# Layer 0 of a graph-attention stack: list and own row of groups 1 to 3 are put in rank order by one indirect transfer out of SBUF

## The chip, the cores and the metric

The kernel runs on one core of a Trainium2 chip. The metric is the device time of one execution in microseconds. Engines are called as in the profile: PE (TensorE), DVE (VectorE), ACT (ScalarE), POOL (GpSimd) and SP (SyncE, which here only issues transfers).

## The reference, cut to what matters

There are 3327 nodes with 256 features and a sparse adjacency matrix, 3327 x 3327 int32, with about 1% of ones and a full diagonal. Four attention layers follow each other, each as `x = layernorm(x + gnn(x, adj))`. Only layer 0 matters here; its scores are not a sum of a row term and a column term, so each pair of neighbours is scored on its own:

```
g_src = x @ W_src.T + b_src                        # one row per node
g_tgt = x @ W_tgt.T + b_tgt
score[i, j] = sum_c a[c] * leaky_relu(g_src[i, c] + g_tgt[j, c])
weights = softmax over j of score, where adj[i, j] != 0
x = layernorm(x + weights @ g_tgt)
```

## The kernel before

**Sparse layer 0.** The function `sparse0` scores a node only against its neighbours. For each node it makes a list of the neighbours' indices (at most 56, `KMAX`), and it then fetches the neighbours' `g_tgt` rows from a table in DRAM, `table_d` (260 numbers a row, 130 KB for 128 nodes), with an indirect transfer on POOL: one instruction fetches one neighbour for each of 128 nodes. This is `gather`, L721, 945 instructions.

**Groups and ranks.** The 26 tiles of 128 nodes are divided into four groups of 4, 7, 9 and 6 tiles (`SETS`). Inside a group the nodes are sorted by their number of neighbours, so that the first tile of a group needs 56 gathers and the last ones fewer than 30 (`LEVELS`). The generator `neighbours(s)` makes the lists of a group: SP loads pieces of the adjacency (`adj_i`, 512 KB, three buffers), ACT converts them (`adj_b`, L484), PE turns them into codes (`v`), DVE takes the largest codes (`cand`, `found`, L514 to L524), and `note` writes a payload of 58 numbers per node: the list, the node's own index in the group, and its diagonal entry. A count of larger keys gives each node's rank, `ranks_i`. It also calls `sources`, which writes the negative `g_src` row of each node.

**Own rows.** Next to the list, each node has an own row of 773 numbers (`OWN`) in `own_d`, in the order of the nodes: the negative `g_src` row, x, and `g_tgt`. Three places write it: `targets`, `sources` and a copy of x.

**Into rank order.** For group 0, `permute` sorts the lists with matmuls. For groups 1 to 3, POOL writes each tile's payload to its ranks in `lists_d` with an indirect transfer (`write_list`, L665), and loads all lists of the group back (`read_lists`, L673). Own rows stay where they are: for each tile in rank order `gather_own` (L709, POOL, 26 instructions) fetches the 128 own rows by the index in the list.

**What is done with them.** `lay_out` copies the own `g_src` row to PSUM (`minus_ps`, ACT). `score` (DVE, L741 and L747) scores up to four neighbours at once. `weights` makes the softmax weights. `combine` scales the gathered rows (ACT, L794) and adds them up on PE (L797), which frees the gather's buffer. `add_input` adds x. `put_back` (POOL, L834) writes the sum to the node's place in `sums_d`, and `take` loads it.

**Order.** Gathers are cut into parts of up to 4; there are 245 parts. The program goes through the parts in steps, one for each part q. POOL's gathers of part q + 8 (`LEAD`) are written beside the scores of part q, and there are 22 buffers of four rows (`TURNS`). `at_step(q, f)` puts f at step q. `once_placed(q, f)` puts f where the gathers of part q are written. `owed` spreads the making of the next group's lists over the steps before. Group 1 starts at part 41, group 2 at part 106 and group 3 at part 188. Work in the list `between` (the list writes and the sums) is taken one piece after every second gather. The order on PE, DVE, ACT and POOL is the order of the program. The order on SP is chosen when the kernel is built. Each engine issues in its own order, and an instruction whose wait isn't over holds what is behind it.

## Time and profile before

| | |
|---|---|
| median of 3 runs | 3092.57 us (3083.05 to 3094.05) |
| the profiled execution, its own time | 3086.17 us |
| its span, first to last instruction | 3084.3 us |
| busy time of PE, DVE, ACT, POOL | 2371.3, 2131.5, 872.9, 1017.5 us |
| layer 0: first and last gather of POOL | 145.8 and 1440.0 us |
| POOL's instructions there: gathers, own gathers, list writes, list loads, sums | 945, 26, 22, 3, 26 |

The profile shows one execution. A line of a group names the source line, the engine, the operation, output<-input, how often, then busy time and mean ns of one, then the idle time of the engine just before these instructions and what ended it. A transfer's instruction ends when it is issued; its landing is told apart, as the time from issue to landing. "issue" means that the engine waited for nothing that the profile shows.

### The profile page before, as it was taken

What the parts mean: (1) busy time and instruction counts of PE and PEld (TensorE: products, weight loads), DVE (VectorE), ACT (ScalarE), POOL (GpSimd) and SP (SyncE); (2) the same over time, 40 slices, a digit from 0 to 9 for tenths busy, and PEclk for the clock granted to TensorE, in tenths of its full rate; (3) what the DMA queues carried; (4) which work ended last, traced back from release to release, by engine and by line L of the source; (5) the groups of instructions that cost most, each with busy time, mean ns of one, the idle gap of its engine ahead of it and who ended that gap; (6) DMA issues with size and microseconds to landing.
All of it is one profiled execution on the core that took longest, in us unless ns stands there. A gap on an engine that the chain in (4) does not pass through costs nothing.

```text
span 3084.3 us, 45518 instructions
## 1 busy us (share of the span) xinstructions
PE 2371.3 (77%) x16077; PEld 1302.9 (42%) x16098; DVE 2131.5 (69%) x5525; ACT 872.9 (28%) x2426; POOL 1017.5 (33%) x1073
## 2 busy tenths in 40 slices
PE   5747657544456432646799999989999999999996
PEld 2313223222222111313688888874434545434332
DVE  3499997776778536654355531129888889899997
ACT  2226545433344322535234421110110110120110
POOL 0077777777777777775000000000000000000000
PEclk8657868776777666868999999999999999999998
DMA  6676675455644435543776643331212212212211
GB/s 181 178 186 189 190 177 171 128 139 147 151 127 116 114 105 118 138 109 95 231 247 204 198 122 92 106 124 46 70 43 72 70 45 71 67 46 61 57 47 45
DMA packets 193029, 372.04 MB, mean 121 GB/s; under 512 B 38992, under 2 KB 135201, under 8 KB 191770
## 3 DMA queue, kind: packets, MB, share of 16 engines
q1 hardware_dynamic: 107648, 176.03, 20.1%
q0 software_dynamic: 51520, 156.84, 19.8%
q10 hardware_dynamic: 33626, 36.18, 3.4%
q8 instruction: 130, 2.13, 0.3%
q14 instruction: 105, 0.86, 0.1%
HBM read 326.21 MB, written 46.12 MB: 121 GB/s over the span
## 4 chain that ended last, share of the span: by engine, by line
PE 46%; DVE 4%; DMA 2%; issue 0%; ACT 0%; SPq 0%; POOL 0%; DVEq 0%; POOLq 0%; ACTq 0%
PE acc L1493 18%; PE acc L1446 16%; PE acc L1501 9%; PE misc L1292 3%; DVE e L1362 2%; DMA at<-at_d 1%; DMA at_i<-in_adj_t_dram 0%; PE misc L1389 0%; PE misc L1575 0%; PE misc L1536 0%; DMA dst<-in_l_a_dram 0%; DVE stats L1653 0%; DVE h L1651 0%; DVE both L1648 0%; DVE h L248 0%
## 5 line engine op out<-in xcount | busy, mean ns | idle before, releaser
L721 POOL DMA_INDIRECT g<-table_d,lst x945 | 900.4, 953 | 306.8 <-issue 255.5
L1362 DVE SCALAR_TENSOR_TENSOR e<-rate,feat,at 128x896 f32<-128x896 f32 (+4 forms) x832 | 843.9, 1079 | 80.9 <-PE acc L1501 70.0
L797 PE MATMUL acc<-g,ident 128*128 128x512 f32 x958 | 524.7, 694 | 341.8 <-ACT g L794 299.5
L1493 PE MATMUL acc<-e,feat 128*32 128x384 f32 (+2 forms) x6656 | 690.2, 516 | 7.3 <-DVE h L1466 4.5
L797 PEld LDWEIGHTS acc<-g,ident 128*128 128x128 f32 x958 | 205.1, 224 | 577.9 <-ACT g L794 442.9
L741 DVE TENSOR_TENSOR y<-g,minus_ps 128x1028 f32<-128x1028 f32 (+2 forms) x245 | 288.9, 1179 | 220.0 <-DMA g<-table_d,lst 203.2
L1493 PEld LDWEIGHTS acc<-e,feat 128*32 128x32 f32 x6656 | 258.4, 110 | 347.6 <-issue 235.8
L794 ACT ACTIVATE g<-g,w 128x256 f32<-128x256 f32 x945 | 389.1, 495 | 16.0 <-issue 8.6
L1501 PE MATMUL acc<-e,feat 128*32 128x384 f32 (+3 forms) x3328 | 376.0, 512 | 0.0
L747 DVE SCALAR_TENSOR_TENSOR y<-y,a_ps 128x257 f32<-128x257 f32 x945 | 342.7, 418 | 7.5
L1446 PE MATMUL acc<-feat,e 128*128 128x257 f32 (+2 forms) x1352 | 304.1, 382 | 15.5 <-DMA at_i<-in_adj_t_dram 13.2
L1446 PEld LDWEIGHTS acc<-feat,e 128*128 128x128 f32 (+2 forms) x1352 | 255.4, 191 | 53.3 <-issue 14.2
L242 POOL TENSOR_TENSOR rstds<-rstds,minus_half 128x7 f32<-128x7 f32 (+1 forms) x12 | 19.7, 1645 | 775.9 <-DVE rstds L241 775.9
L494 PE MATMUL v<-code,leads 65*128 65x512 bf16 (+1 forms) x182 | 84.2, 464 | 221.0 <-DVE cand L514 178.4
L1446 PE MATMUL acc<-feat,at 128*128 128x257 bf16 (+2 forms) x2028 | 237.8, 274 | 4.2 <-DMA at<-at_d 4.0
L1446 PEld LDWEIGHTS <-at 128*128 128x128 bf16 (+2 forms) x2028 | 198.8, 99 | 37.9 <-DMA at<-at_d 4.5
L1501 PEld LDWEIGHTS acc<-e,feat 128*32 128x32 f32 (+1 forms) x3328 | 139.0, 110 | 154.8 <-issue 131.2
L514 DVE MAX8 cand<-v 128x8 f32<-128x104 f32 (+2 forms) x858 | 159.1, 259 | 53.5 <-PE v L497 41.4
L1362 DVE SCALAR_TENSOR_TENSOR e<-rate,feat,at_i 128x896 f32<-128x896 f32 (+2 forms) x104 | 111.6, 1080 | 73.3 <-DMA at_i<-in_adj_t_dram 51.9
L1342 POOL DMA_DIRECT2D rate3b_d<-rate_rows x4 | 2.1, 526 | 468.9 <-ACT rate_rows L1341 468.9
L494 PEld LDWEIGHTS <-leads 65*128 65x128 bf16 x182 | 19.8, 109 | 287.2 <-DVE cand L514 232.4
L1379 ACT CAST at<-at_i 128x896 bf16<-128x896 int32 (+2 forms) x104 | 92.0, 885 | 107.8 <-DMA at_i<-in_adj_t_dram 90.0
(201 smaller groups left out, 1788.3 us busy)
## 6 DMA issues: line engine op xcount, KB each, us to landing
adj_i<-in_adj_dram SPq DMA_DIRECT2D x75, 512.0 KB, 4.4
at<-at_d SPq DMA_DIRECT2D x150, 224.0 KB, 2.5
at_i<-in_adj_t_dram SPq DMA_DIRECT2D x50, 448.0 KB, 4.5
g<-table_d,lst POOLq DMA_INDIRECT x945, 2.8
at<-at_d SPq DMA_DIRECT2D x75, 192.0 KB, 2.3
at<-at_d SPq DMA_DIRECT2D x75, 191.8 KB, 2.3
at_d<-at ACTq DMA_DIRECT2D x50, 224.0 KB, 4.2
at_i<-in_adj_t_dram SPq DMA_DIRECT2D x25, 384.0 KB, 3.3
```

Of the source, the lines that this page charges most:

```text
L494: nc.tensor.matmul(v[:, :w], leads[:, b, :], code[:, :w], start=True, stop=False)
L514: nc.vector.max(spread[:, c0 + c, :], view(v[:, :w]))
L721: nc.gpsimd.indirect_dma_start(out=g[:, k - k0, :], out_offset=None, in_=table_d[:, :], in_offset=bass.IndirectOffsetOnAxis(ap=entry["lst" ...
L741: nc.vector.tensor_tensor(y, rows, minus_src[:, None, :].to_broadcast([P, m, dim + 1]), op=ALU.max)
L747: nc.vector.scalar_tensor_tensor(y, y, 1.0, a_ps[:, : dim + 1], op0=ALU.mult, op1=ALU.mult, accum_out=sc)
L794: nc.scalar.activation(rows, rows, AF.Copy, scale=w[:, k : k + 1])
L797: nc.tensor.matmul(dst, ident, rows, start=start, stop=stop)
L1292: nc.tensor.matmul(pacc[:pn, : dim + self.extra], ht[:, k, :pn], self.weight[:, k, :], start=(k == 0), stop=(k == kc - 1),)
L1362: nc.vector.scalar_tensor_tensor(e[:pn, : c1 - c0], self.rate[b][:pn, h_of, : c1 - c0], q, at[:pn, : c1 - c0], op0=ALU.max, op1=ALU.mult,)
L1446: nc.tensor.matmul(accs[s][:pn, : dim + 1], a[:pj, s * P : s * P + pn], f[:pj, : dim + 1], start=(j == 0 and part == 0), stop=(j == nt - 1 ...
L1493: nc.tensor.matmul(accs[x][p][q : q + 32, : hi - lo], f[:pj, at0 : at0 + 32], es[at0 // hd][:pj, lo:hi], start=(j == 0), stop=(j == nt - 1),)
L1501: nc.tensor.matmul(accs[x][pairs][h_of * 32 : (h_of + 1) * 32, : hi - lo], f[:pj, dim + h_of : dim + h_of + 1].to_broadcast([pj, 32]), es[ ...
```

## The change

The payload of groups 1 to 3 no longer goes to its rank by itself. `note` writes it (from ACT) behind the node's own row in `own_d`, whose rows grow from 773 to 831 numbers. `write_list` becomes two halves: SP loads a whole tile of 128 rows of 831 numbers into a tile `stage` in SBUF (two buffers), and POOL writes this tile to its ranks in `lists_d` with one indirect transfer; the load of tile t is written one piece of `between` ahead of the write of tile t. `read_lists` is issued by SP and loads the lists as floats into a buffer of the same two (`read`), and a new `keep_lists` on ACT converts them. `gather_own` becomes a plain load of 128 consecutive rows by SP for groups 1 to 3; group 0 keeps its four indirect gathers. The payload has 3 buffers instead of one per tile, and `own` has 3 instead of 4. The list writes start two steps earlier than before, and the load of the lists one step.

The diff:

```diff
@@ -44,6 +44,7 @@
 AT_X = 257
 AT_TGT = 513
 OWN = 773
+AT_LIST = OWN
 
 
 @with_exitstack
@@ -366,7 +367,7 @@
             own_d = []
             for s, size in enumerate(SETS):
                 lo, hi = starts[s] * P, min(n, (starts[s] + size) * P)
-                own_d.append(dram.tile([size * P, OWN], F32, name=f"own{s}_d"))
+                own_d.append(dram.tile([size * P, OWN if s == 0 else AT_LIST + KMAX + 2], F32, name=f"own{s}_d"))
                 if s == 0:
                     copy_rows(nc.gpsimd, own_d[s][: hi - lo, AT_X : AT_X + dim], x[lo:hi, :])
 
@@ -403,7 +404,7 @@
                 yield
                 nc.scalar.copy(row[:pn], pt[:pn, :ROW])
                 nc.scalar.dma_start(table_d[1 + it * P : 1 + it * P + pn, :], row[:pn])
-                nc.scalar.dma_start(own_rows(it)[:, AT_TGT:], row)
+                nc.scalar.dma_start(own_rows(it)[:, AT_TGT:OWN], row)
                 yield
 
             def sources(it):
@@ -422,7 +423,7 @@
                 yield
 
             lists_d = [
-                dram.tile([size * P, KMAX + 2], U32, name=f"lists{s}_d")
+                dram.tile([size * P, AT_LIST + KMAX + 2], F32, name=f"lists{s}_d")
                 for s, size in enumerate(SETS)
             ]
             sums_d = [
@@ -529,7 +530,7 @@
                 def note(t):
                     it, found = starts[s] + t, founds.pop(t)
                     payload = io0.tile(
-                        [P, KMAX + 2], U32 if s else F32, tag=f"pay{t}", name="payload", bufs=1
+                        [P, KMAX + 2], F32, tag=f"pay{t}" if s == 0 else "pay", name="payload", bufs=1 if s == 0 else 3
                     )
                     nc.vector.tensor_scalar(
                         payload[:, :KMAX], found, 1.0 - BASE, 0.0, op0=ALU.add, op1=ALU.max
@@ -542,6 +543,8 @@
                         junk, found, BASE - 0.5, 0.0, op0=ALU.is_lt, op1=ALU.add,
                         accum_out=missing,
                     )
+                    if s:
+                        nc.scalar.dma_start(own_d[s][t * P : (t + 1) * P, AT_LIST:], payload)
 
                 def key(t):
                     it = starts[s] + t
@@ -660,20 +663,35 @@
                 )
                 listed[0] = lst
 
+            staged = {}
+
             def write_list(s, t):
-                ranks_i, payloads = placed[s]
-                nc.gpsimd.indirect_dma_start(
-                    out=lists_d[s][:, :],
-                    out_offset=bass.IndirectOffsetOnAxis(ap=ranks_i[:, t : t + 1], axis=0),
-                    in_=payloads[t][:, :], in_offset=None,
-                )
+                if t < SETS[s]:
+                    stage = staged[s, t] = io0.tile([P, AT_LIST + KMAX + 2], F32, tag="stage", name="stage")
+                    nc.sync.dma_start(stage, own_d[s][t * P : (t + 1) * P, :])
+                if t:
+                    ranks_i, _ = placed[s]
+                    nc.gpsimd.indirect_dma_start(
+                        out=lists_d[s][:, :],
+                        out_offset=bass.IndirectOffsetOnAxis(ap=ranks_i[:, t - 1 : t], axis=0),
+                        in_=staged.pop((s, t - 1))[:, :], in_offset=None,
+                    )
 
             def read_lists(s):
+                while between:
+                    between.pop(0)()
+                read = io0.tile([P, AT_LIST + KMAX + 2], F32, tag="stage", name="read")
+                read = read[:, : max(SETS) * (KMAX + 2)].rearrange("p (t k) -> p t k", k=KMAX + 2)
+                nc.sync.dma_start(
+                    read[:, : SETS[s], :],
+                    lists_d[s].rearrange("(t p) k -> p t k", p=P)[:, :, AT_LIST:],
+                )
                 lst = io0.tile([P, max(SETS), KMAX + 2], U32, tag="lst", name="lst")
-                nc.gpsimd.dma_start(
-                    lst[:, : SETS[s], :], lists_d[s].rearrange("(t p) k -> p t k", p=P)
-                )
                 listed[s] = lst
+                return read
+
+            def keep_lists(s, read):
+                nc.scalar.copy(listed[s][:, : SETS[s], :], read[:, : SETS[s], :])
 
 
             pens = {}
@@ -705,7 +723,10 @@
 
                 entry = held[s, t] = {"g": {}}
                 lst = entry["lst"] = listed[s][:, t, :]
-                own = entry["own"] = io0.tile([P, OWN], F32, tag="own", name="own_of", bufs=4)
+                own = entry["own"] = io0.tile([P, OWN], F32, tag="own", name="own_of", bufs=3)
+                if s:
+                    nc.sync.dma_start(own, lists_d[s][t * P : (t + 1) * P, :OWN])
+                    return
                 nc.gpsimd.indirect_dma_start(
                     out=own[:, :], out_offset=None, in_=own_d[s][:, :],
                     in_offset=bass.IndirectOffsetOnAxis(ap=lst[:, KMAX : KMAX + 1], axis=0),
@@ -979,9 +1000,11 @@
                 if k0 == 0:
                     if key[1] == 0:
                         at_step(q, judge, key[0])
-                        at_step(q, lay_out, *key)
+                        if key[0]:
+                            once_placed(q - 2, gather_own, *key)
+                        at_step(q - 2 if key[0] else q, lay_out, *key)
                     else:
-                        once_placed(q - 3, gather_own, *key)
+                        once_placed(q - 2, gather_own, *key)
                         at_step(q - 2, lay_out, *key)
             for q, key in ends.items():
                 count = len(cuts_of(places[key]))
@@ -1013,9 +1036,12 @@
             ahead, owed, steps = [], {}, 0
             for s in range(1, len(SETS)):
                 at = begins[s] - LEAD - 2
-                at_step(at, read_lists, s)
+                reads = {}
+                at_step(at - 1, lambda s, reads: reads.update({s: read_lists(s)}), s, reads)
+                at_step(at, lambda s, reads: keep_lists(s, reads[s]), s, reads)
+                at -= 2
                 at -= SETS[s] // 2 + 1
-                for it in range(SETS[s]):
+                for it in range(SETS[s] + 1):
                     at_step(at, between.append, lambda s=s, it=it: write_list(s, it))
                 ahead.append(neighbours(s))
                 steps += steps_of(s)
```

More of the change, by code (lines that the diff above doesn't have):

```diff
@@ L661, in permute, with read_lists @@
                 listed[0] = lst
+            staged = {}
             def write_list(s, t):
-                ranks_i, payloads = placed[s]
-                nc.gpsimd.indirect_dma_start(
-                    out=lists_d[s][:, :],
-                    out_offset=bass.IndirectOffsetOnAxis(ap=ranks_i[:, t : t + 1], axis=0),
-                    in_=payloads[t][:, :], in_offset=None,
+                if t < SETS[s]:
[8 more added lines that the diff above has]
+                    )
+            def read_lists(s):
+                while between:
[5 more added lines that the diff above has]
+                    lists_d[s].rearrange("(t p) k -> p t k", p=P)[:, :, AT_LIST:],
                 )
-            def read_lists(s):
                 lst = io0.tile([P, max(SETS), KMAX + 2], U32, tag="lst", name="lst")
-                nc.gpsimd.dma_start(
-                    lst[:, : SETS[s], :], lists_d[s].rearrange("(t p) k -> p t k", p=P)
-                )
                 listed[s] = lst
+                return read
+            def keep_lists(s, read):
+                nc.scalar.copy(listed[s][:, : SETS[s], :], read[:, : SETS[s], :])
             pens = {}
```

## The prediction

> **What bounds the kernel now.** I read the slices first, then the costly groups, then GpSimd's own groups, and last the timeline around one step that the change touches.
>
> ```profile
> PE   5747657544456432646799999989999999999996
> POOL 0077777777777777775000000000000000000000
> DMA  6676675455644435543776643331212212212211
> ```
>
> A slice is 77 us. POOL shows a flat 7 from slice 2 to slice 17, and that plateau is layer 0. The later layers belong to PE and the change does not touch them.
>
> ```profile
> L721 POOL DMA_INDIRECT g<-table_d,lst x945 | 900.4, 953 | 306.8 <-issue 255.5
> L741 DVE TENSOR_TENSOR y<-g,minus_ps 128x1028 f32<-128x1028 f32 (+2 forms) x245 | 288.9, 1179 | 220.0 <-DMA g<-table_d,lst 203.2
> ```
>
> 945 gathers of 953 ns stand 0.30 us apart, and that gap is called "issue": POOL waits for nothing. VectorE waits for the gathers, not they for it. From 145.8 to 1441 us the end of layer 0 is therefore a count of POOL's instructions, 1.26 us each. The groups of POOL say what the others cost:
>
> ```profile
> L834 POOL DMA_INDIRECT sums_d<-hs,lst x26 | 26.2, 1009 | 30.1 <-DVE lost L1048 12.9 <-DVE inv L821 9.9 <-issue 4.3
> L709 POOL DMA_INDIRECT own_of<-own_d,lst x26 | 25.0, 961 | 134.4 <-DVE lst L658 126.9 <-issue 7.2 <-DVE y L741 0.3
> L665 POOL DMA_INDIRECT lists_d<-payload,ranks_i x22 | 22.2, 1007 | 10.4 <-DMA lists_d<-payload,ranks_i 5.2 <-issue 5.2
> L673 POOL DMA_DIRECT2D lst<-lists_d x3 | 3.1, 1030 | 0.0
> ```
>
> An own row is three times as long as a gathered row, yet costs POOL the same. In the third line, 5.2 us of waits for an earlier list write already stand. The timeline of POOL at the end of group 1's writes shows one, and the list's load:
>
> ```profile
> 344.76 0.99 POOL L665 DMA_INDIRECT lists_d<-payload,ranks_i  x1 [0.30 <-issue]
> 346.06 0.97 POOL L721 DMA_INDIRECT g<-table_d,lst  x1 [0.30 <-issue]
> 347.34 0.96 POOL L721 DMA_INDIRECT g<-table_d,lst  x1 [0.31 <-issue]
> 349.19 0.99 POOL L665 DMA_INDIRECT lists_d<-payload,ranks_i  x1 [0.89 <-DMA lists_d<-payload,ranks_i]
> 350.49 0.97 POOL L721 DMA_INDIRECT g<-table_d,lst  x1 [0.30 <-issue]
> 351.77 0.96 POOL L721 DMA_INDIRECT g<-table_d,lst  x1 [0.31 <-issue]
> 352.73 1.08 POOL L673 DMA_DIRECT2D lst<-lists_d  x1
> ```
>
> Unhindered, write follows write after 3.83 us (1.01 + 0.30 and two gathers); here it took 4.43, because the write before had not landed. Landing times, of the own rows, the list writes and the sums in turn, are in the answers by tile:
>
> ```profile
> DMA to landing us min/median/max: 3.7/4.0/6.3
> DMA to landing us min/median/max: 2.2/2.3/5.4
> DMA to landing us min/median/max: 2.4/2.5/9.3
> ```
>
> And two waits, SP's for ScalarE's conversion of the adjacency and VectorE's for gathers, inside the stretch from 130 to 1420 us:
>
> ```profile
> SPq L126 <- ACT adj_b L484: 481.4, 64, 45.4
> DVE y L741 <- DMA g<-table_d,lst: 189.6, 85, 9.5
> ```
>
> **What the Trainium skill says.** "Perfetto Trace Analysis", section "DMA Instruction — SWDGE (GPSIMD)": the profile ends such an instruction when the descriptors are made, not when data has landed. The trace agrees: 961 ns for own rows (386 KB), 953 for gathers (130 KB). So I price the larger list write at 1.01 us of POOL too. "DMA: Bandwidth & Descriptors", section "Anatomy of one DMA — SWDGE (gpsimd) path": 2.0 us plus bytes/436e3 per transfer. For the list write (29 KB) and the sums (128 KB) the fit gives 2.1 and 2.3 us against 2.3 and 2.5 measured; for an own row it gives 2.9 against 4.0, so for large rows I use the trace. Its section "Rules for kernel authors" says that a DMA reading what another wrote must wait for that one's completion, and that spreading transfers over issuing engines adds no bandwidth. The first is L665's wait above; the second no run here shows alone.
>
> **The change part by part.** The sum is made against the profiled execution: 3086.17 us with a span of 3084.3. The median of the runs is 3092.57, 6.4 higher, so I carry a difference over.
>
> Removed from POOL. The built order has 22 own gathers fewer (group 0 keeps its four): 22 x 1.26 = 27.7 us. Three list loads leave: from 351.77 the next gather would have come at 353.03 and came at 354.11, 1.08 each, 3.2 us. The waits of L665 beyond plain issue are 5.2 - 5 x 0.30 = 3.7 us; I take them out to count all waits anew. Gross: 34.6 us, all on the path.
>
> Added on POOL. The 22 list writes stay, two gathers apart, but each now moves 128 x 831 x 4 bytes = 416 KB instead of 29. Each waits for the write before it to land and for its stage, which SP loads. There are two stage buffers, so SP's load for write k+2 waits for write k to land. In the built order the first two stages of each group are loaded far ahead; the third needs the first write. So a loop of write, landing, load, landing spans two writes. Write landing: extrapolating list to sums (0.2 us for 99 KB) gives 3.1, the own gather with 30 KB more gives 4.1; I take 4.1, since rows of this length landed so. Load: adjacency pieces land in 2.5 us at 127.5 KB and 4.4 at 512 KB, interpolated 3.9; around 300 to 360 us the large ones took 5.0, so 4.5 there. With two wake-ups of 0.25 us the loop is 8.5 to 9.1 us, 4.3 to 4.6 a write. Chance delays, such as the list writes' 5.4, are added to a wait and never subtracted: I take 4.7, so 0.9 above 3.83. The first write of each group waits for none of this: 19 x 0.9 = 17 us. Bounds: below, 3.1 + 3.7 + 0.5 = 7.3 per pair, no stall, 0 us. Above, per write two gathers, a write, a load and half an adjacency piece are 1347 KB; the stretch 146 to 1441 moved 144 GB/s at a DMA share of 0.55, so 262 GB/s when busy: 5.3 us. With queueing 5.7, a stall of 1.9, is 36 us. A gain from the larger write itself is excluded: its descriptors are as many as before.
>
> Added on SP: 22 stage loads, 22 own loads, three list loads, each an issue of about 0.4 us, of no account by itself. But SP issues in order. The third stage load of group 2 stands ahead of three adjacency pieces which before were issued at 640.1, 643.7 and 658.8; they now wait for writes that begin near 665. What is late next is scanning of group 3's adjacency, on ScalarE, PE and VectorE. POOL's cover is the gather buffers: 22, filled 8 parts ahead.
>
> Added on ScalarE: three copies of the list (under 1 us), 22 payload issues, and the wait of that copy. It stands at step 96 for group 2. ScalarE was through with that step at 660.4; the last write would be at about 702 (nine, 4.7 apart), landed at 706, loaded at 711. ScalarE stands some 50 us, and with it VectorE from about 671 to 713, because the next tile's `minus` and the conversions are queued behind the copy. VectorE had some 25 us of work there. From 720 to 800 it was busy 58.6 of 80 us, so it catches up 21; 4 remain at the end of the group's first tile. POOL's own margin: the first part of that tile was scaled at 801-802, its buffer was wanted 31 us later, at 833.6. In group 1 the hold is about 330 to 354, margin 28 us; group 3's falls on 28.6 us for which VectorE stood already (1114 to 1143). So I cost the hold at nothing, covered by those margins; if cover is gone, it costs POOL what exceeds them.
>
> POOL's first gather of a new group now waits for the copy: write, load and copy need some 10 us after the last write; 13, 11 and 16 gathers and some sums lie between (14 us at least). Own rows for later tiles come ahead on SP with 3 buffers instead of 4; the shortest tiles make that load wait for `add_input` three tiles back, at most five steps of 5 us, needed eight steps later. Nothing.
>
> Sum: -34.6 + 17 = -17.6 us, 3068.6 against 3086.17; on the median about 3076.
>
> **The rivals.** (a) No stall: landings fit under two gathers. For it, the small list writes waited only 5 times in 22; against it, 14 times the bytes. -34.6: 3058. (b) The DMA engines are the bound in the write windows: 36 us of stalls eat the gain. For it, DMA shares of 0.54 in the first window before anything is added; against it, 0.44 and 0.33 in the other two. About +1: 3094. (c) Slower: SP's queue becomes the releaser. Between the stage loads of groups 1 and 2 stand eight adjacency or x pieces, and a wait of SP for a conversion is 481.4/64 = 7.5 us on average. Each piece that holds a stage beyond the landing it overlaps (about 1.5 us spare) costs POOL 6 us: 8 x 6 = 48, so +30: 3122. It decides from about 2 us per piece for the gain to vanish, 4 us for a measurable loss. Against it: ScalarE and VectorE run ahead of POOL in the program, and SP reached those pieces before the writes. A hold of ScalarE past the margins adds to the same side. That the change does not do what it says can be left out: the built order shows the 22 gathers gone.
>
> **How the numbers follow.** A measurement of this kernel can tell about 0.5%, 15.5 us. Case (a) 0.15, faster. My case 0.45: stalls of 8 to 27 us, gain 8 to 27, two thirds of it beyond 15.5, so 0.30 faster and 0.15 same. Case (b) 0.20, same. Case (c) 0.20, slower. Together 0.45, 0.35, 0.20. The range runs from (a) with 3 us of scatter in the runs, 3055, to half of (c), 3108; my case alone is 3065 to 3085.
>
> **What would show it.** Right: POOL's groups list 4 own gathers; the list write's idle time is 10 to 30 us, released by the stage or by the earlier write; gathers keep 0.30 us; POOL's last gather comes near 1424 instead of 1440; ScalarE waits some 50 us for `read`. Wrong: list writes waiting over 2 us each, a stage load released by ScalarE rather than by a write, gathers waiting for PE (a full ring of buffers), or a first gather waiting for the list's copy.

## The result, and the profile after

The kernel after takes 3089.07 us (median of 12 executions, 3078.82 to 3105.65), the kernel before 3091.97 (12 executions): ratio 0.999, 95% interval 0.9975 to 1.0005. The forecast was 3076, a gain of 16 us; what came is 3 us between the medians, and the interval runs from a gain of 8 us to a loss of 1.5.

The first measurement and the last series of experiments found the kernel before at 3090 us, the four series between them at 3513 to 3536 us, so kernels are compared only within their series, and the two levels are kept apart by these numbers.

The profiled execution of after took 3105.65 us (span 3103.9), the longest of its 12. Its groups on GpSimd, in the form line, engine, operation, tiles, count, then busy time and mean ns of one, then idle time in front of them and what ended it:

```profile
L742 POOL DMA_INDIRECT g<-table_d,lst x945 | 897.7, 950 | 322.2 <-issue 255.7 <-DMA g<-table_d,lst 25.9 <-DMA table_d<-row 19.6
L674 POOL DMA_INDIRECT lists_d<-stage,ranks_i x22 | 21.9, 996 | 35.5 <-DMA lists_d<-stage,ranks_i 31.3 <-issue 2.7 <-DVE ranks_i L619 1.6
L730 POOL DMA_INDIRECT own_of<-own_d,lst x4 | 3.9, 976 | 143.7 <-DVE lst L661 137.1 <-DVE hs L844 6.0 <-issue 0.6
```

The work removed is gone: four own gathers are left of 26, and no list load. One list write costs GpSimd 996 ns, as before (1007), though it moves 416 KB and not 29. But the idle time in front of the 22 writes rose from 10.4 to 35.5 us, and 31.3 of it ended when an earlier list write landed. The third line holds a second new wait: 6.0 us of an own gather for `hs`. The timeline of GpSimd near the end of group 1's writes (start, duration, engine, line, idle time before) shows what the writes look like:

```profile
363.74 0.99 POOL L674 DMA_INDIRECT lists_d<-stage,ranks_i  x1 [0.62 <-DMA lists_d<-stage,ranks_i]
365.03 0.97 POOL L742 DMA_INDIRECT g<-table_d,lst  x1 [0.30 <-issue]
366.31 0.95 POOL L742 DMA_INDIRECT g<-table_d,lst  x1 [0.30 <-issue]
371.23 0.99 POOL L674 DMA_INDIRECT lists_d<-stage,ranks_i  x1 [3.97 <-DMA lists_d<-stage,ranks_i]
372.53 0.97 POOL L742 DMA_INDIRECT g<-table_d,lst  x1 [0.30 <-issue]
373.80 0.95 POOL L742 DMA_INDIRECT g<-table_d,lst  x1 [0.30 <-issue]
376.31 0.99 POOL L674 DMA_INDIRECT lists_d<-stage,ranks_i  x1 [1.56 <-DMA lists_d<-stage,ranks_i]
```

From write to write 7.49 and 5.08 us, where two gathers and a write need 3.83. Over all pairs within a group the mean distance is 5.39 us (4.04 before). The landing of these writes, in the answer by their line, was 2.2/2.3/5.2 before (the 5.4 that the prediction names is from a view that takes in the list loads too) and is now:

```profile
DMA to landing us min/median/max: 3.2/4.9/6.4
```

Three waits bear on the other steps of the prediction (waiting engine and line, what it waits for, total us, times, longest; SP's queue is SPq):

```profile
ACT lst L694 <- DMA read<-lists_d: 126.6, 3, 61.4
POOL g L742 <- PE acc L818: 9.7, 32, 0.3
SPq L671 <- DMA lists_d<-stage,ranks_i: 181.7, 16, 67.9
```

ScalarE does stand at the list's copy, up to 61.4 us. GpSimd does not feel it: its 32 waits for a gather buffer are of 0.3 us, which is plain issue. SP's stage loads stand for the landing of list writes, not for ScalarE's conversions (two more waits of theirs, 15.1 us together, are for a payload to land in `own_d`).

**The balance from first to last gather** (idle time beyond 0.30 us per instruction counted as wait) comes out of the timelines of GpSimd. The stretch ends where the last gather starts, and that gather is still counted among the instructions, so instructions and waits together exceed it by some 1.2 us. The waits include small negative terms, of instructions that follow with less than 0.30 us, so the columns to their right can exceed them. The last two rows are kernels of the experiments below. All four are at 3090 us:

| kernel | first gather at | stretch | instructions with 0.30 us each | waits | of list writes | of gathers | of own gathers |
|---|---|---|---|---|---|---|---|
| before | 145.8 | 1294.2 | 1283.6 | 11.8 | 3.8 | 9.7 | 0.0 |
| after | 161.7 | 1300.7 | 1248.7 | 53.3 | 28.9 | 19.4 | 5.7 |
| after_c (after again) | 139.9 | 1296.2 | 1248.9 | 48.6 | 28.3 | 15.1 | 5.9 |
| gross_order | 149.8 | 1264.5 | 1248.9 | 16.8 | 5.2 | 12.3 | 0.0 |

35 us of instructions left, 37 to 42 us of waits came. Some 3 of the 35 us are not instructions removed: the gathers took 950 ns each instead of 953 in the lower three kernels, which nobody had forecast and nothing here explains. In the same three kernels 1.3 us of the list writes' waits, at the first write of group 1, are for `ranks_i`; the rest is for landings. That the first gather came at 161.7 in the first profile is no part of the change: the same kernel had it at 139.9 in another execution, and the kernel before had it at 160.8 in one (before_p, below).

### The profile page after: what moved, and what is told of

It reads as the page before. It is cut to its first block, busy times and chain, and to the rows that moved or that the text cites. A ratio compares the mean times of both kernels' runs of the same rounds, so it can differ in the third digit from the quotient of the medians.

```text
span 3103.9 us, 45643 instructions
## 1 busy us (share of the span) xinstructions
PE 2369.9 (76%) x16076; PEld 1305.4 (42%) x16098; DVE 2130.2 (69%) x5525; ACT 872.3 (28%) x2429; POOL 990.0 (32%) x1048
## 4 chain that ended last, share of the span: by engine, by line
PE 46%; DVE 4%; DMA 1%; issue 1%; ACT 0%; SPq 0%; POOL 0%; DVEq 0%; POOLq 0%
PE acc L1519 18%; PE acc L1472 16%; PE acc L1527 9%; PE misc L1318 2%; DVE e L1388 2%; DMA at<-at_d 1%; PE misc L1415 0%; PE misc L1601 0%; PE misc L1562 0%; DMA dst<-in_l_a_dram 0%; DMA at_i<-in_adj_t_dram 0%; DVE stats L1679 0%; DVE h L1677 0%; DVE both L1674 0%; DVE h L249 0%
## 5 line engine op out<-in xcount | busy, mean ns | idle before, releaser
L818 PE MATMUL acc<-g,ident 128*128 128x512 f32 x958 | 508.4, 675 | 446.6 <-ACT g L815 394.9
L818 PEld LDWEIGHTS acc<-g,ident 128*128 128x128 f32 x958 | 198.8, 217 | 673.4 <-ACT g L815 545.4
L485 ACT ACTIVATE adj_b<-adj_i 128x1024 bf16<-128x1024 int32 (+1 forms) x104 | 92.3, 888 | 148.1 <-issue 55.5
```

Of the source, the lines that this page charges most:

```text
L485: nc.scalar.activation(adj_b[:pn, : hi - lo], loaded.pop((t, p))[:pn, : hi - lo], AF.Copy, accum_out=counts[:pn, it, p : p + 1],)
L818: nc.tensor.matmul(dst, ident, rows, start=start, stop=stop)
```

## The experiments

Theory: where GpSimd is the bound, the 35 us of its instructions are really saved, and come back as waits of the list writes, of one own gather and of some gathers. Rivals: GpSimd's instruction count is not what ends layer 0; ScalarE's hold costs the time; the stage loads or SP's queue, not the landing, slow the writes.

### First series (before at 3513.14 us)

**after_again** is the changed kernel unaltered.

> The changed kernel once more, unaltered, for a second profile beside the runs of this series. Theory: the 31 us of GpSimd instructions that left (22 own gathers, three list loads) are saved, and come back on GpSimd as waits: list writes waiting for the write before them or their stage about 25 to 30 us beyond plain issue (28.9 in the first profile against 3.6 before), the own gather of group 0's last tile waiting about 6 us for `hs` (3 own buffers), gathers waiting for earlier transfers 5 to 15 us. First to last gather then 1290 to 1302 us, time 3080 to 3100. The late first gather of the first profile (161.7 us against 145.8) is the granted clock of TensorE in the first 160 us, not the change: with another clock there it should come at another time, 140 to 165. Rival: the late start belongs to the change, and comes again at 160 or later whatever the clock.

3465.28 us, ratio 0.986 (0.9831 to 0.9888). First gather at 154.9. The expected times were missed by far, because layer 0 ran otherwise here. Three views tell how: the group of gathers in this kernel, a line of VectorE's timeline in the kernel before at 3090 us, and VectorE's timeline in this kernel at 247 us:

```profile
L742 POOL DMA_INDIRECT g<-table_d,lst x945 | 897.4, 950 | 523.7 <-issue 293.9 <-PE acc L818 153.6 <-remote 21.5
```

```profile
199.90 1.63 DVE L514 MAX8 cand<-v 128x8 f32<-128x104 f32 x9
```

```profile
248.65 0.28 DVE L515 MAX8 cand<-v 128x8 f32<-128x104 f32 x1 [1.11 <-issue]
250.06 0.28 DVE L515 MAX8 cand<-v 128x8 f32<-128x104 f32 x1 [1.13 <-issue]
251.45 0.28 DVE L515 MAX8 cand<-v 128x8 f32<-128x104 f32 x1 [1.11 <-issue]
252.86 0.27 DVE L515 MAX8 cand<-v 128x8 f32<-128x96 f32 x1 [1.13 <-issue]
```

Where nine such instructions took 1.63 us before, one of 0.28 us starts every 1.4 us here, without a wait that the profile shows. TensorE and ScalarE start late too, while GpSimd goes on at 1.26 us per gather until its buffers are full and it stands for TensorE (153.6 us; 9.7 in the first profile). So here the other engines set the pace of layer 0. GpSimd waits 393.4 us in the stretch, and 411.0 in the kernel before at this level (before_p, below). List writes still waited 24.8 us for landings.

**noown**, in the kernel before:

```diff
                 own = entry["own"] = io0.tile([P, OWN], F32, tag="own", ...)
+                if s:
+                    nc.sync.dma_start(own, own_d[s][t * P : (t + 1) * P, :])
+                    return
```

> The kernel before, with one edit: the own rows of groups 1 to 3 are loaded by SyncE in node order instead of gathered by GpSimd in rank order (so the own rows belong to other nodes than the lists: part of the computation is changed). List writes, list loads and all buffers are those of before. It shows what the removal of 22 own gathers is worth when nothing is added to GpSimd. Theory (the end of layer 0 is a count of GpSimd's instructions): 22 x 1.26 = 27.7 us less from first to last gather, time about 3064, ratio 0.990 to 0.992. Rival (something else sets the end of layer 0, VectorE or the transfers, and GpSimd's instructions were cover): less than 10 us, ratio 0.997 or more, with gathers waiting for buffers instead.

3482.85 us, 0.9927 (0.9899 to 0.9954): about 26 us by the ratio and 30 by the medians, near the 27.7 although GpSimd waits some 400 us for others. Waits in the stretch: 402.0 us. What GpSimd does is not mere cover even here.

**small**, in the changed kernel:

```diff
-                dram.tile([size * P, AT_LIST + KMAX + 2], F32, name=f"lists{s}_d")
+                dram.tile([size * P, KMAX + 2], F32, name=f"lists{s}_d")
...
-                        in_=staged.pop((s, t - 1))[:, :], in_offset=None,
+                        in_=staged.pop((s, t - 1))[:, AT_LIST:], in_offset=None,
...
-                    lists_d[s].rearrange("(t p) k -> p t k", p=P)[:, :, AT_LIST:],
+                    lists_d[s].rearrange("(t p) k -> p t k", p=P),
...
-                    nc.sync.dma_start(own, lists_d[s][t * P : (t + 1) * P, :OWN])
+                    nc.sync.dma_start(own, own_d[s][t * P : (t + 1) * P, :OWN])
```

> The changed kernel, but the indirect list write moves only the 58 list columns (29 KB instead of 416 KB), and the own rows are then loaded in node order (part of the computation is changed). Stages, their two buffers, the stage loads of 416 KB, the copy of the list on ScalarE and the order of everything stay. Theory A (stalls come from the landing of the large write, 4.9 us median, which both the next write and the stage load two later wait for): landing falls to about 2.3 to 2.5 us, the waits of list writes from 28.9 us to 3 to 8, time about 22 us under the changed kernel, ratio to before about 0.991 to 0.993. Rival B (the stage loads through two buffers, or SyncE's queue in front of them, set the pace): waits of 15 us or more stay, time within 10 us of the changed kernel. Rival C (the hold of ScalarE at the list's copy costs the time, not the writes): waits fall and the time does not.

3461.44 us, 0.9852 (0.9825 to 0.9879), 4 us under after_again. The groups of list writes, first of after_again, then of small:

```profile
L674 POOL DMA_INDIRECT lists_d<-stage,ranks_i x22 | 21.9, 996 | 54.5 <-DMA lists_d<-stage,ranks_i 24.8 <-DVE ranks_i L619 24.3 <-issue 5.3
```

```profile
L674 POOL DMA_INDIRECT lists_d<-stage,ranks_i x22 | 21.9, 997 | 38.8 <-DVE ranks_i L619 24.3 <-issue 10.3 <-DMA lists_d<-stage,ranks_i 4.3
```

Stages of 416 KB, their two buffers and SP's loads are the same in both, and the wait for landings fell from 24.8 to 4.3 us. So a write waits for the wide write before it to land, and neither for its stage nor for SP's queue. What makes that landing long is not told apart: the edit also takes 387 KB of each write's traffic away. The time hardly followed, as rival C had it, but the cause that it names, ScalarE's hold, is taken out in nohold below without gain. That GpSimd waits elsewhere for what it gains at this level is the likelier reason; it is argued, not shown.

**spread23**, in the changed kernel:

```diff
-                    if k % 2 and between:
+                    if k % (4 if s else 2) == (3 if s else 1) and between:
...
-                at -= SETS[s] // 2 + 1
+                at -= SETS[s] + 2 if s > 1 else SETS[s] // 2 + 1
```

> The changed kernel, but while groups 1 and 2 are gathered (writes of groups 2 and 3) a list write comes after every fourth gather instead of every second, and begins so many steps earlier; the same bytes, buffers and instructions. Group 1's writes are left as they are. Unhindered, write then follows write after about 6.4 us, over the 4.9 us landing and the loop of two writes through the stage buffers. Theory A (the pace of two gathers is too short for the landing): the waits of the writes of groups 2 and 3, 20 us of the 28.9 in the changed kernel's profile, fall to 0 to 5; time 12 to 18 us under the changed kernel. Rival (the transfers as a whole are the bound in these stretches, so the wait moves to the gathers): writes wait less, gathers more, time as the changed kernel, within 5 us. A loss of 5 us or more would say that ranks and scanning, wanted some 25 us earlier, come too late.

3471.29 us, 0.9873 (0.984 to 0.9905), no faster than after_again. Waits for landings fell to 9.2 us, most of it in group 1's untouched writes; in groups 2 and 3 write follows write mostly after 6.3 us, the plain distance. The first write of group 2 stands 28.4 us for VectorE, but it stood 24.3 in after_again already, so this explains 4 us at most.

### Second series (before at 3519.02 us)

The same three kernels and one new.

> The kernel before with the own rows of groups 1 to 3 loaded by SyncE in node order (part of the computation is changed: own rows belong to other nodes than the lists), once more, because the first series fell on a chip on which the kernel before took 3513 us and VectorE, TensorE and ScalarE were short of instructions in layer 0, so that GpSimd waited for them. If this series is at about 3090 us for the kernel before: theory, 22 x 1.26 = 27.7 us less from first to last gather (1294 to about 1267), time about 3064, ratio 0.990 to 0.992. Rival (something other than GpSimd sets the end of layer 0 even then): ratio 0.997 or more. If it is at 3513 again: 0.993 as in the first series.

3487.61 us, 0.9905 (0.988 to 0.993).

> The changed kernel with a list write of only the 58 list columns (own rows then loaded in node order, part of the computation is changed), once more, for the same reason. On a chip at about 3090 us: theory A (the stalls come from the landing of the large write, 4.9 us median in the first profile of the changed kernel), waits of list writes from 28.9 us to 3 to 8, ratio 0.991 to 0.993. Rival B (stage loads through two buffers or SyncE's queue): waits of 15 us or more stay, ratio 0.996 or more. Rival C (ScalarE's hold at the list's copy costs the time): waits fall, ratio stays at 0.998 to 1.000.

3462.99 us, 0.982 (0.9795 to 0.9846); list writes wait 8.0 us for landings.

> The changed kernel with the list writes of groups 2 and 3 after every fourth gather instead of every second, once more, for the same reason. On a chip at about 3090 us: theory A, the waits of the writes of groups 2 and 3 fall from about 17 us together to 0 to 5 (the first series showed one write of group 3 waiting 1.06 us and one of group 2 that waited for its ranks), ratio about 0.994. Rival (transfers as a whole are the bound there): gathers wait more instead, ratio 0.999 as the changed kernel.

3476.18 us, 0.9877 (0.9856 to 0.9898); 10.3 us for landings.

**combo** is spread23 with one edit more:

```diff
-                        once_placed(q - 2, gather_own, *key)
+                        once_placed(q - 2 if key[0] else q, gather_own, *key)
```

> The changed kernel with two edits: list writes of groups 2 and 3 after every fourth gather, and the own gathers of group 0 issued two parts later (at the first gather of their tile instead of two parts ahead), so that the last one no longer waits for the buffer that `add_input` of the first tile frees. On a chip at about 3090 us: theory, the 6.0 us wait of the own gather of tile 3 of group 0 goes (0 to 1 us left) on top of what the spread writes save: ratio about 0.992. Rival: the own row then comes too late for ScalarE's `minus`, VectorE lags and the wait comes back at the gather buffers: ratio as the spread alone.

3477.59 us, 0.9894 (0.9872 to 0.9917). The own gather's wait for `hs`, beyond plain issue, fell from 12.3 us in spread23_b to 7.9, not to 0 to 1. Neither repair makes the kernel faster at this level.

### Third series (before at 3535.79 us)

> The kernel before, unaltered, for a profile on the chip of this series. If it is the chip of the earlier series (3513 us): in layer 0 VectorE, ScalarE and TensorE are short of instructions as they were in the changed kernel there, GpSimd waits for them some 400 us from first to last gather, and that stretch is 1665 to 1700 us against 1294 in the first profile. If instead it takes about 3090 us: first to last gather 1290 to 1298 us, list writes waiting 3 to 4 us beyond plain issue, first gather between 139 and 162 us.

One execution, 3537.76 us. First to last gather 1692.7 us, waits 411.0: the same state of things as in after_again.

> The changed kernel, unaltered, beside it on the same chip. On the chip of the earlier series: first to last gather 1640 us or near, 30 to 50 us under the kernel before. At about 3090 us: 1290 to 1302 us, list writes waiting 20 to 30 us beyond plain issue, one own gather 6 us, gathers 10 to 20 us for earlier transfers.

One execution, 3474.85 us. Stretch 1653.1 us, waits 403.4. From before_p to after_p the instructions fell by 32 us and the waits by 8.

**nohold**, in the changed kernel, with the payload kept as U32:

```diff
-                        nc.scalar.dma_start(own_d[s][t * P : (t + 1) * P, AT_LIST:], payload)
+                        nc.scalar.dma_start(own_d[s][t * P : (t + 1) * P, AT_LIST:], payload[:, :].bitcast(F32))
...
-                    read[:, : SETS[s], :],
+                    lst[:, : SETS[s], :].bitcast(F32),
...
-                nc.scalar.copy(listed[s][:, : SETS[s], :], read[:, : SETS[s], :])
+                pass
```

> The changed kernel, but the list's numbers travel as unsigned integers' bits in the wide row, so that the list is loaded by SyncE straight into its place and ScalarE copies nothing: the three waits of ScalarE for `read` (126.6 us in the first profile) go, with the waits of VectorE behind them. All else stays. Prediction's step: the hold costs nothing, because GpSimd's gather buffers cover it; time within 5 us of the changed kernel. Rival: the hold makes VectorE late and costs 10 us or more; the time falls by that.

3483.71 us, 0.9853 (0.9824 to 0.9882), against 0.986 for the changed kernel in the first series and one execution of 3474.85 us in this one. ScalarE's waits for the list are gone (46.4 us in after_again), and nothing is gained. At 3090 us it was not run; there the waits of GpSimd for buffers, 0.3 us each, say the same.

**gross** is noown with one more edit, `nc.sync.dma_start` for `nc.gpsimd.dma_start` in `read_lists`.

> The kernel before without 22 own gathers and three list loads on GpSimd: own rows come by SyncE in node order, lists by SyncE (part of the computation is changed: own rows belong to other nodes than the lists). Nothing is added to GpSimd. It is the gross of the prediction's sum, 27.7 + 3.2 = 30.9 us: ratio 0.990. Where VectorE and the others set the pace (the 3513 us chip) a theory in which GpSimd's instructions don't count gives 0.997 or more; noown gave 0.9927 and 0.9905 there, so 0.989 to 0.993 is expected.

3509.29 us, 0.993 (0.9906 to 0.9953): 26 us by the medians, as expected, and again not the 10 us or less of a theory in which GpSimd's instructions don't count.

### Fourth series: light kernels (before at 3517.03 us)

The edit, in each of the four kernels; l_small and l_spread have the edits of small and spread23 besides:

```diff
                 (s, t), k0, k1 = parts[q]
+                if k0:
+                    return
...
+                    nc.vector.memset(entry["sc"], 0.0)
...
-                for k in range(k0, k1):
-                    scale(g[:, k - k0, :dim], k)
+                if i == 0:
+                    scale(g[:, 0, :dim], 0)
-                pairs = [g[:, k : k + 2, :dim] for k in range(0, m - 1, 2)]
+                pairs = [g[:, k : k + 2, :dim] for k in range(0, m - 1, 2)][:1]
...
-                    if m % 2:
-                        add_up(acc[:, 1, :], g[:, m - 1, :dim])
```

> A light form of the kernel before, to make GpSimd the bound of layer 0 again on this chip: VectorE scores only the first part of each tile, ScalarE scales only its first row, TensorE adds only the first pair of rows of each part (that much of the computation is left out). All gathers, scans, list writes, sums and buffers stay. Theory: GpSimd waits only for ranks and a few transfers, first to last gather 1295 to 1360 us against 1693 in the full kernel, with list writes waiting 3 to 5 us for transfers. Rival: the short supply of instructions hits GpSimd itself or the scans as much as before, and the stretch stays over 1500 us; then these four runs say nothing on the bound.

3310.11 us, 0.9419 (0.9393 to 0.9444). Stretch 1508.0 us, waits 226.0: GpSimd still waits for the other engines, so the aim was missed, and by the rival these four runs say nothing on the bound.

> The same light form of the changed kernel. Theory (where GpSimd is the bound, the 34.4 us of instructions removed come back as waits of the list writes, the own buffer and the gathers): list writes wait 20 to 30 us for transfers, and the time is -15 to +5 us of the light kernel before. Rival 1 (the waits are absorbed by other waits here too): -30 to -50 us, as the full kernels differ on this chip. Rival 2 (the first chip's result was the late start alone): -30 us.

3268.73 us, 0.929 (0.9266 to 0.9314), 41 us under l_before, as rival 1 says. Waits 217.5 us; list writes waited 17.5 for landings and one of them 9.5 for its stage.

> The light form of the changed kernel whose list write moves only the 58 list columns (own rows then in node order; parts of the computation are changed and left out). Theory A (landing of the large write is what the next write waits for): list writes wait 2 to 8 us for transfers, time 15 to 25 us under the light changed kernel. Rival B (the large stage loads through two buffers set the pace): waits stay over 15 us and the time is that of the light changed kernel.

3274.42 us, 0.9315 (0.9296 to 0.9334), 6 us over l_after where 15 to 25 under it were expected. The waits for landings are gone, but two writes stood 16.4 us for their stage.

> The light form of the changed kernel with list writes of groups 2 and 3 after every fourth gather. Theory A: waits of these groups' writes for transfers fall from 15 to 18 us to 0 to 5, time 10 to 18 us under the light changed kernel. Rival (transfers as a whole are the bound): gathers wait instead, time within 5 us of it.

3290.74 us, 0.9369 (0.9342 to 0.9396), 22 us over l_after where 10 to 18 under it were expected; two of its writes stood 30.2 us for their stage.

These four agree with one thing: where GpSimd waits for other engines anyway, the removed instructions were gained, and taking the landing waits away gained nothing. Why the one counts there and the other does not, they don't show. Nor do they tell what happens where GpSimd doesn't wait. And they warn of the repairs: a stage that comes late can take the place of the landing.

### Fifth series (before at 3090.68 us)

**gross_order** is gross with the order of the changed kernel, the emptying of `between` ahead of the list's load included:

```diff
-                        at_step(q, lay_out, *key)
-                    else:
-                        once_placed(q - 3, gather_own, *key)
+                        if key[0]:
+                            once_placed(q - 2, gather_own, *key)
+                        at_step(q - 2 if key[0] else q, lay_out, *key)
+                    else:
+                        once_placed(q - 2, gather_own, *key)
...
-                at_step(at, read_lists, s)
+                at_step(at - 1, read_lists, s)
+                at -= 2
```

> The kernel before with nothing added to GpSimd: 22 own gathers and three list loads gone from it (own rows by SyncE in node order, so part of the computation is changed), and with the changed kernel's order besides: own rows and `minus` two parts ahead, also for the first tile of a group, list writes two steps earlier, the list's load one step earlier. In the earlier series on the 3513 us chip gross gave 0.993, the changed kernel 0.986 and 0.982 to 0.985 with a small write, though both add waits. Theory: the rest comes from this order, because it takes waits off the engines that set the pace there: ratio 0.983 to 0.988. Rival: the order is of no account, and the rest has another source (three own buffers, the wide rows, scatter from series to series): ratio 0.991 to 0.995. At about 3090 us for the kernel before: 0.990 in either case.

3060.19 us, 0.9898 (0.9882 to 0.9915): 30.5 us less than before (26 to 36 by the interval), beside the 30.9 worked out for it. Its list writes, still of 29 KB, and its own gathers:

```profile
L665 POOL DMA_INDIRECT lists_d<-payload,ranks_i x22 | 22.0, 1001 | 11.8 <-issue 5.8 <-DMA lists_d<-payload,ranks_i 4.4 <-DVE ranks_i L616 1.5
L714 POOL DMA_INDIRECT own_of<-own_d,lst x4 | 3.9, 977 | 130.4 <-DVE lst L658 129.5 <-issue 0.9
```

> The changed kernel, unaltered, on the same chip in the same series, for that comparison. On the 3513 us chip: 0.983 to 0.989, with first to last gather near 1645 us and waits of GpSimd near 400 us. At about 3090 us: 0.9975 to 1.0005 as first measured, with waits of GpSimd of 40 to 55 us from first to last gather against 12 in the kernel before.

3090.56 us, ratio 1.0 (0.9986 to 1.0015). On the same chip, in the same series, the gross is there and the changed kernel has none of it. Its groups and its landing (by the line of the list write):

```profile
L674 POOL DMA_INDIRECT lists_d<-stage,ranks_i x22 | 21.9, 996 | 34.9 <-DMA lists_d<-stage,ranks_i 31.0 <-issue 2.3 <-DVE ranks_i L619 1.6
L730 POOL DMA_INDIRECT own_of<-own_d,lst x4 | 3.9, 976 | 127.3 <-DVE lst L661 120.5 <-DVE hs L844 6.2 <-issue 0.6
```

```profile
DMA to landing us min/median/max: 4.3/5.6/6.5
```

Both kernels have 1248.9 us of instructions in the stretch, and it is 31.7 us longer in after_c: list writes 23.1, own gather 5.9, gathers 2.8 (rounded, from the table). That is the 30.4 us between their medians. The two profiled executions themselves lie only 18 us apart: after_c's began its gathers 9.9 us earlier and ended 3.6 us sooner after the last. The timeline of after_c in group 2 shows what a write waits for:

```profile
682.15 0.32 SPq L671 DMA_DIRECT2D stage<-own_d  x1
682.90 0.99 POOL L674 DMA_INDIRECT lists_d<-stage,ranks_i  x1 [3.25 <-DMA lists_d<-stage,ranks_i]
687.75 0.32 SPq L671 DMA_DIRECT2D stage<-own_d  x1
688.00 0.99 POOL L674 DMA_INDIRECT lists_d<-stage,ranks_i  x1 [1.58 <-DMA lists_d<-stage,ranks_i]
```

One landing releases both SP's load and, 0.25 to 0.75 us later, the next write. The load of 682.15 is for the write after the next, of 688.00; with 3.4 us to land it is there long before. In groups 1 and 2 of both profiles of the changed kernel at 3090 us, 4.8 us or more lie between the load of a stage and its write, and these loads land in 3.1 to 4.5 us. So where writes wait, their distance is one landing and a wake-up, and the stage is not in it.

## Why the prediction was wrong, step by step

- **Gross gain, 34.6 us: right.** 30.9 us of it are own gathers and list loads; gross_order, in which they are gone and nothing is added, gained 30.5. Its stretch is 29.7 us shorter. That it fits to half a microsecond is luck: its gathers are 3 us shorter in all, and it waits 5 us more. The rest of the 34.6, the small writes' old waits, stays there.
- **Stall of the list writes, "19 x 0.9 = 17 us": the step that failed, by the landing of the wide write, priced at 4.1 us.** Measured: 28.9 and 28.3 us in the two profiles, 27 to 28 of them for landings, about 1.4 a write and not 0.9. The wide writes landed in 4.9 and 5.6 us (medians of the two profiles), and write followed write after 5.4 us on the mean, against 3.83 unhindered. The pace was also worked out from the wrong chain. It was priced as write, landing, load, landing over two writes, 4.3 to 4.6 us a write, with chance delays 4.7. In the trace the chain is write, landing, next write: each write waits for the one before it, though they go to different rows. That wait was named in the prediction, but with a landing of 4.1 us, borrowed from own gathers of nearly this size, and a wake-up of 0.25 to 0.75 us it comes to 4.35 to 4.85 us, about what the loop gives, and dropped out. So the wrong chain alone would have done little harm; the landing did. The gathers' landing did not carry over to scattered writes beside stage loads. The fit of the Trainium skill ("DMA: Bandwidth & Descriptors", section "Anatomy of one DMA — SWDGE (gpsimd) path": 2.0 us plus bytes/436e3) gives an estimate of 3.0 us for 416 KB; here the measurement decides, and it is 4.9 to 5.6. small shows that the waits go with the wide write; in spread23 a pace of 6.3 us covers the landing.
- **A reading that was wrong: L665's wait.** The prediction quotes a rule on a transfer that reads what another wrote, and calls the wait of L665 a case of it. L665 only writes: there a write waits for an earlier write to other rows of the same tensor. It is this wait that grew.
- **Three own buffers instead of four, "Nothing": missed by 6 us.** The argument was made for rows that SP loads. The four rows of group 0 are still gathered by GpSimd, and the last of them stood for `add_input` of the first tile (5.7 and 5.9 us beyond plain issue). gross_order, with four buffers and the same order, has no such wait. It lies on the engine that is the bound.
- **Gathers "keep 0.30 us": nearly.** Their waits were 9.7 us before, 12.3 in gross_order, 15.1 and 19.4 in the changed kernel. 3 to 10 us were not priced. That the added transfers cause them was only argued.
- **ScalarE's hold, "at nothing": right.** It was longer than the 50 us said (61.4), and the gather buffers covered it: no gather waited for a buffer beyond 0.3 us. nohold gained nothing, though at 3513 us.
- **The first gather of a group and the list's copy, no cost: right**; no gather waits for that copy.
- **Rival (c), SP's queue: not borne out.** Stage loads were released by writes. Rival (a), no stall, is refuted by the trace. Rival (b), 36 us of stalls, gave the right time, and its pace of 5.3 to 5.7 us a write was the right one. Its mechanism, transfer engines at their limit, is not what the trace shows: in after_c they were busy to 0.76, 0.76 and 0.72 in the three windows of list writes (320 to 354, 666 to 711, 1103 to 1128 us), against 0.54, 0.44 and 0.33 before. But that this load lengthens the landing, to 4.9 and 5.6 us, is not excluded: small takes most of the write's bytes away with the wait, so it can't tell. And (b) did not have the 6 us of the own buffer, nor the gathers' waits.

The sum with measured terms, from after_c: 34.7 us of instructions less, 36.8 us of waits more, so +2 us for the stretch. That is within 0.5%, as measured. The sum forecast -17.6. The measured 3089 lies in the range of 3055 to 3108, but outside the 3065 to 3085 of the prediction's own case; it is the rivals that kept it in the range.

Three things stay open. What makes the wide write's landing 4.9 to 5.6 us, its size, its scattered rows or the traffic beside it, was not told apart. At 3513 to 3536 us the changed kernel gained 48 us (after_again) and 61 (after_p, one execution), and gross 26; the run meant to tell its order apart fell in a series at 3090 us, so the source of the rest isn't shown. And small, spread23, combo and nohold weren't run at 3090 us. That a repair of the landing waits would bring back up to 23 us there, and a fourth own buffer 6, is an estimate from the table above, and the light kernels show that a repair can bring waits for the stage instead; no version that computes the whole and beats both kernels was measured.

## What to carry to other kernels

An indirect transfer of 128 rows cost its issuing engine no more here at 416 KB than at 29, but each waits for the one before it on the same tensor, and so its landing time is the pace: measure or bound that landing for the very operation, a scattered write under load, before pricing the overlap. A buffer taken away to pay for another has to be checked at each of its users, above all at the one on the engine that is the bound. And look for what a new wait delays: at 3090 us, where GpSimd is the bound, the waits ate the whole gain, while at 3513 us, where it waits for others anyway, no run shows that they cost anything.

## What the runs showed that was not expected

- The same kernel took 3090 us or 3513 to 3536 us in different series. In after_again, at 3513 us, VectorE had stretches in which instructions that wait for nothing the profile shows started 0.70 us or a multiple of it apart, while GpSimd kept its 1.26 us per gather. In the same timeline TensorE stood 51 us up to 237.5 us and ScalarE 7 us up to 238.6, and about 13 us after GpSimd had run out of buffers and stopped, VectorE was back at its usual pace. Each series of experiments ran on another chip, and the mean granted clock of TensorE was about 0.82 at the upper level against 0.86 to 0.87 at 3090 us. Whether the chip makes the level, what slows the engines, and whether GpSimd's gathers do, was not settled.
- The issue cost of an indirect transfer on GpSimd did not follow its size: 1007 ns for 29 KB, 996 for 416 KB. Its landing was longer: 2.3 us against 4.9 to 5.6, beside more traffic.
